# A graph layer's edge sort on one Trainium2 core: six of thirteen tiles sorted into shared places in blocks 8 to 40, sums begun later, and their one-hots made by ScalarE

## The chip, the cores and the metric

The kernel runs on one core of a Trainium2 chip. The core has five engines that run side by side, each with its own instruction stream: TensorE (PE; its weight loads are listed as PEld), VectorE (DVE), ScalarE (ACT), GpSimd (POOL) and SyncE (SP, which here only issues DMAs). They wait for one another through semaphores. SBUF is the core's working memory with 128 partitions; PSUM is the small memory that TensorE writes to. The metric is the device time of one execution in microseconds, as the median of several. Before the change it is 1903.76 us (three runs, 1901.55 to 1904.29).

## The reference: a message-passing layer over 206,250 edges

There are 6250 nodes with 64 features and 206,250 edges (in the order of `dst`) with 64 features. Cut to what matters:

```python
msg = concat([x[dst], edge_attr], axis=1)          # 206250 x 128
h = relu(msg @ W1a.T + b1a) @ W1b.T + b1b
sums = segment_sum(h, src, num_segments=6250)
agg = sums / maximum(counts, 1)[:, None]
z = relu(concat([x, agg], axis=1) @ W2a.T + b2a) @ W2b.T + b2b
out = concat([z, x], axis=1) @ Wr.T + br
result = layernorm(x + out)
```

So each edge makes a row of 128 hidden values, and the rows are summed by `src`, which is in no order. The second linear layer of the edge network is applied after the sum.

## The kernel before

**Tiles and blocks.** An edge tile is 128 edges; 13 tiles (`NG`, `BLK`) make a block; there are 124 blocks. Nodes fall into 49 bins of 128 (`NB`). The main loop (L1481) runs over blocks `k`. PE, ACT, DVE and SP run exactly in the order in which the loop's body issues their instructions (`manual_schedule`, L1468); POOL's order is left to the framework.

**A block's way.** `group` (L1138) loads, three blocks ahead, the block's edge features into the upper 64 partitions of a `rhs` buffer and the places of its `dst` nodes in a window of 64 nodes. `columns` (L1162) turns these places into one-hot columns in the lower 64 partitions, two blocks ahead, with one DVE comparison (L1171). `hidden` (L1186) multiplies tile by tile with the block's weights (TensorE) and stores the relu in `orow` (ACT, L1196), in parts of 4, 3, 3 and 3 tiles; the last part is issued later in the body than the others.

**The sort.** `bins_of` (L934) marks on DVE, two blocks ahead, which bin each edge's `src` falls into and keeps running counts by a scan (L983); two columns are carried from the block before (L969). `counts_of` (L988) adds over partitions with TensorE. `slots` (L1001) makes from this each edge's row number in DRAM. `scatter` (L1198) then sends a tile's 128 rows of 130 numbers to their places in `rows`, with one indirect DMA of POOL per tile (L1228). It is called `LEAD` = 2 blocks later.

**Joined tiles.** In blocks 5 to 103 (`joined`), the first three tiles take another way: `quads` (L1051) gives each bin's edges of these tiles whole places of four rows, `join_marks` (L1097) makes one-hot marks (DVE, L1099), `join` (L1104) moves the rows to their places with 12 matmuls (24 records) and ACT copies them into a buffer `mrow` (three of them, in `shared`), `join_places` (L1125) finds the place's index one block later, and one indirect DMA (L1203) sends all three tiles to `quads` in DRAM. Such a block has 1 + 10 scatters, others have 13.

**The sums.** Epochs of 104, 12, 4 and 4 blocks use three row buffers in turn. Once enough blocks are scattered that every bin surely has t full tiles (a step; `FULL`, `FULLQ`), SP reads those tiles back (`read`, L1285), DVE makes one-hots of the node numbers (`nodes_of`, L1310), PE sums per node (`summed`, L1332), and DVE (ACT for the first step) adds to `part` (`collect`, L1390). Groups of at most three bins or 12 tiles are spread over the blocks `LATE` = 4 after their step. `clear` (L1266) fills those places that may stay empty with padding rows, by DMAs on ACT's queue, in blocks 5 to 12 for the first epoch and the joins. `nodes_ahead` (L1451) computes the node network's part that needs no sums, four bins at a time, from block `PRE` = 14 on. Behind the last block the last sums and the node network run.

In a block's body the order is: marks, counts of the next block, three parts of `hidden`, `columns` and `bins_of` two blocks ahead, `join_places` of the last block, `nodes_ahead`, `clear`, first half of a sum, `slots` of the next block, last part of `hidden`, `join`, the rest of the sums, `scatter` of block `k - 2`.

Of the kernel before, what the change touches and what calls it, by code (L numbers as in the profile page):

```python
# [451 lines left out]
EPOCHS = (104, 12, 4, 4)  # L452
# [3 lines left out]
FULL = (4, 7, 10, 12, 15, 18)  # L456
# [6 lines left out]
PRE = 14  # L463
# [7 lines left out]
JOIN_FROM, JOIN_TO = 5, 104  # L471
FULLQ = (2, 3, 5)
# [10 lines left out]
def fast_path(  # L483
# [47 lines left out]
    DIR = BLK - JOIN  # L531
# [14 lines left out]
    def joined(k):  # L546
        return JOIN_FROM <= k < JOIN_TO
# [4 lines left out]
    def edges_of(b, n, first=0):  # L552


        tiles = sum(DIR if joined(k) else BLK for k in range(first, first + n))
# [8 lines left out]
    def quads_of(b, n):  # L564
# [4 lines left out]
        n = sum(joined(k) for k in range(n))  # L569
# [15 lines left out]
    for e, n in enumerate(EPOCHS):  # L585
# [46 lines left out]
    NREST = P * JOIN_TO  # L632
# [101 lines left out]
    with (  # L734
# [12 lines left out]
        slm = by_slot.enter_context(tc.tile_pool(name="joinp", bufs=3))  # L747
# [60 lines left out]
        nc.vector.tensor_copy(ramp, iota_i)  # L808
        in_win = steady[:, P : P + 1]
# [21 lines left out]
        starts_at(False)  # L831
# [11 lines left out]
        z_ps = steady[:, P + 2 + HALF * TJ :][:, :JOIN]  # L843
        assert DIR % 2 == 0 and DIR + JOIN == BLK == 13
# [13 lines left out]
        bases = [const.tile([P, 2 * HALF + 2], F32, name=f"bases{i}") for i in range(2)]  # L858
        most_q = const.tile([P, 1], F32, name="most_q")
        qplace = const.tile([P, JOIN_TO], F32, name="qplace")  # L860
        qidx = const.tile([P, JOIN_TO], I32, name="qidx")

        def join_consts():
# [7 lines left out]
            for t in bases:  # L871
                nc.vector.memset(t, 0.0)
            nc.vector.memset(most_q, 0.0)
            at = slp.tile([P, 1], F32, name="at")
            nc.vector.tensor_scalar(at, part_f, float(NQ), None, op0=ALU.add)
            nc.vector.tensor_scalar(qplace, ramp[:, :JOIN_TO], float(P), at, op0=ALU.mult, op1=ALU.add)
# [57 lines left out]
        def bins_of(k):  # L934
# [4 lines left out]
            if joined(k):  # L939
                return bins_joined(k, ep_, c0)  # L940
            if k == JOIN_TO:
                starts_at(False)
            oh = slp.tile([P, 2 * HALF * T], BF16, name="bins", padded_shape=[P, 2 * HALF * TJ])
            had = slp.tile([P, 2 * HALF * T], BF16, name="had", padded_shape=[P, 2 * HALF * TJ])
            by_bin = oh.rearrange("p (b t) -> p b t", t=T)
            was = none_b if k == ep_.first else state["had"][:, :, BLK]
            nc.vector.tensor_tensor(by_bin[:, :, 0], was, on[:, : 2 * HALF * T].rearrange("p (b t) -> p b t", t=T)[:, :, 1], op=ALU.mult)
# [808 lines left out]
```

## Time and profile before

| | |
|---|---|
| median of three runs | 1903.76 us (1901.55 to 1904.29) |
| the profiled execution's own time | 1908.35 us |
| its span, first to last instruction | 1906.5 us |
| instructions in the span | 31966 |
| mean granted clock of TensorE | 0.882 |
| DMA traffic | 392.17 MB, 206 GB/s on average |

A line of the page's groups, or of the view that groups by line, gives the source line, engine, operation, what is written and read (out<-in), the shape, the count, the busy microseconds, the mean nanoseconds of one, and the idle time of the engine just before it with what ended it. In the timeline a row begins with its start and length in us. In the windows view each row is a stretch of the span, with the busy us and the number of instructions of each engine, the granted share of TensorE's clock, the mean busy share of the DMA engines, and GB/s. fp32 matmuls appear as two records each. "Issue" is idle time for which the profile shows no wait.

### The profile page before, as it was taken

To read this page: it belongs to the slowest core of one execution; us is meant where nothing else is said; L and a number is where in the kernel's file an instruction comes from. 1 tells how busy PE (TensorE), PEld (TensorE's weight loads), DVE (VectorE), ACT (ScalarE), POOL (GpSimd) and SP (SyncE) were. 2 spreads that over 40 slices of the span, in tenths; PEclk is the share of its full clock that TensorE was granted. 3 is DMA by queue.
4 is the path that set the end of the run, shared out by engine and by line. 5 is a ranking of instruction groups with operands and counts; after the bars stand their busy time and mean duration, and the time that the engine had idled before them with its cause. 6 is when DMAs were issued, how large, how long until landed. Compare 5 with 4: busy or idle time off the path is not lost.

```text
span 1906.5 us, 31966 instructions
## 1 busy us (share of the span) xinstructions
PE 1450.4 (76%) x10729; PEld 1375.1 (72%) x10729; DVE 1592.4 (84%) x3348; ACT 419.1 (22%) x1203; POOL 1361.9 (71%) x1431
## 2 busy tenths in 40 slices
PE   5564677778877787787877677777788888889976
PEld 5553677768777677777777567666787887879964
DVE  7395676689998889899999888788999988898976
ACT  2221222222222222222122121212122111111035
POOL 5777776777777777777777777777777777777710
PEclk8786777788888889899899888888999999999988
DMA  8899645668665556566665545555567988888951
GB/s 191 229 350 364 215 151 168 206 193 263 199 193 163 177 173 205 168 200 207 187 195 153 158 142 164 157 169 176 184 203 222 292 251 268 246 274 273 313 155 31
DMA packets 221897, 392.17 MB, mean 206 GB/s; under 512 B 43201, under 2 KB 148020, under 8 KB 221596
## 3 DMA queue, kind: packets, MB, share of 16 engines
q1 hardware_dynamic: 139626, 227.02, 41.4%
q0 software_dynamic: 50000, 113.97, 18.3%
q10 hardware_dynamic: 32098, 49.04, 7.6%
q8 instruction: 88, 1.44, 0.3%
q14 instruction: 85, 0.70, 0.1%
HBM read 225.10 MB, written 164.77 MB: 204 GB/s over the span
## 4 chain that ended last, share of the span: by engine, by line
DVE 31%; DMA 25%; PE 24%; POOL 8%; issue 7%; ACT 2%; ACTq 2%; SPq 0%; POOLq 0%; DVEq 0%
DMA rows<-orow,rowidx 14%; PE sum_ps L1342 9%; POOL rows L1228 8%; PE h_ps L1193 7%; DMA quads<-shared,qidx 6%; DVE rhs L1171 5%; PE h_ps L1114 5%; DVE shared L1099 5%; DVE had L983 4%; DVE oh L1323 4%; DMA quads<-padrow 3%; DVE bins L977 2%; DVE part L1398 2%; DVE row L1016 1%; PE h_ps L1464 1%
## 5 line engine op out<-in xcount | busy, mean ns | idle before, releaser
L1228 POOL DMA_INDIRECT rows<-orow,rowidx x1315 | 1264.2, 961 | 427.2 <-issue 284.8
L1193 PE MATMUL h_ps<-mv,rhs 128*128 128x128 f32 x3224 | 502.3, 314 | 238.3 <-ACT of_q L1120 172.8
L1193 PEld LDWEIGHTS h_ps<-mv,rhs 128*128 128x128 f32 x3224 | 471.4, 226 | 263.5 <-ACT of_q L1120 184.7
L1342 PE MATMUL sum_ps<-rt,oh 128*128 128x129 f32 x4106 | 549.8, 291 | 83.0 <-DVE part L1398 63.2
L1342 PEld LDWEIGHTS sum_ps<-rt,oh 128*128 128x128 f32 x4106 | 523.5, 206 | 94.0 <-DVE part L1398 72.0
L1196 ACT ACTIVATE orow<-h_ps 128x512 f32<-128x512 f32 x496 | 253.0, 521 | 452.5 <-PE h_ps L1193 397.6
L1114 PE MATMUL h_ps<-orow,shared 128*128 128x130 f32 (+1 forms) x2376 | 302.0, 285 | 0.0
L1114 PEld LDWEIGHTS h_ps<-orow,shared 128*128 128x128 f32 x2376 | 295.9, 202 | 0.0
L1099 DVE TENSOR_TENSOR shared<-quad_ramp,ramp 128x1536 f32<-128x1536 f32 x99 | 173.1, 1749 | 78.5 <-PE h_ps L1114 78.5
L1171 DVE TENSOR_TENSOR rhs<-rhs,ramp 64x1664 f32<-64x1664 bf16 x116 | 219.4, 1892 | 3.6
L1118 ACT COPY shared<-h_ps 128x260 f32<-128x260 f32 x198 | 71.9, 383 | 651.8 <-DMA quads<-shared,qidx 573.3
L1323 DVE TENSOR_TENSOR oh<-ramp,rt 128x768 f32<-128x768 f32 (+2 forms) x266 | 209.7, 810 | 0.0
L1398 DVE TENSOR_TENSOR part<-part,sum_ps 128x258 f32<-128x258 f32 (+2 forms) x265 | 124.5, 470 | 72.1 <-PE sum_ps L1342 70.7
L983 DVE TENSOR_TENSOR_SCAN had<-ramp,bins 128x750 bf16<-128x750 bf16 x99 | 170.2, 1719 | 3.4
L1323 DVE TENSOR_TENSOR oh<-ramp,node 128x768 f32<-128x768 f32 (+3 forms) x133 | 118.9, 894 | 4.6
L1203 POOL DMA_INDIRECT quads<-shared,qidx x99 | 95.2, 961 | 30.2 <-issue 14.6
L997 PE MATMUL cnt_ps<-had,one_w 128*128 128x375 bf16 (+1 forms) x248 | 83.5, 340 | 42.8 <-DVE at_q L1065 34.7
L977 DVE TENSOR_TENSOR bins<-ramp,hi 128x500 bf16<-128x500 f32 x198 | 107.9, 585 | 0.0
L1016 DVE TENSOR_REDUCE row<-cnt_ps 128x10 f32<-128x500 f32 (+1 forms) x124 | 86.6, 699 | 2.3 <-PE cnt_ps L998 2.2
L998 PE MATMUL cnt_ps<-bins,before_w 128*128 128x350 bf16 (+1 forms) x248 | 84.6, 344 | 0.0
L1487 ACT CAST orow<-lo 128x13 f32<-128x13 bf16 x124 | 28.5, 230 | 249.5 <-DMA rows<-orow,rowidx 229.0
L998 PEld LDWEIGHTS <-before_w 128*128 128x128 bf16 x248 | 25.3, 102 | 56.0 <-issue 47.4
(153 smaller groups left out, 864.5 us busy)
## 6 DMA issues: line engine op xcount, KB each, us to landing
rt<-rows SPq DMA_DIRECT2D x192, 390.0 KB
rhs<-in_edgeT SPq DMA_DIRECT2D x124, 416.0 KB
rhs<-relt SPq DMA_DIRECT2D x116, 208.0 KB
rows<-orow,rowidx POOLq DMA_INDIRECT x1315
rows<-padrow ACTq DMA_DIRECT2D x4, 3900.0 KB
rt<-rows SPq DMA_DIRECT2D x48, 325.0 KB
rt<-rows SPq DMA_DIRECT2D x50, 260.0 KB
rt<-quads SPq DMA_DIRECT2D x49, 260.0 KB
```

The costliest lines, as they stand in the source:

```text
L977: nc.vector.tensor_tensor(by_bin[:, :, t0 : t0 + n], ramp[:, : 2 * HALF, None].to_broadcast([P, 2 * HALF, n]), hi[:, None, c : c + n].to_b ...
L983: nc.vector.tensor_tensor_scan(had, on, oh, 0.0, op0=ALU.mult, op1=ALU.add)
L998: nc.tensor.matmul(v[:, :, : t - 1], before_w, oh[:, b, 1:], start=False, stop=True)
L1099: nc.vector.tensor_tensor(m, quad_ramp.rearrange("p g q -> p (g q)")[:, None, :].to_broadcast([P, JOIN, QUAD * P]), z_ps[:, :, None].to_br ...
L1114: nc.tensor.matmul(ps[:, i, :w], m[:, t, (g0 + i) * P : (g0 + i + 1) * P], orow[:, t, :w], start=t == 0, stop=t == JOIN - 1,)
L1171: nc.vector.tensor_tensor(rhs[D:, :].rearrange("p (h e) -> p h e", h=2), rel, in_win[D:, :, None].to_broadcast([WIN, 2, NG * P // 2]), op= ...
L1193: done[k, c] = nc.tensor.matmul(ps[:, j, :], rhs[:, c * P : (c + 1) * P], m, start=True, stop=True).ins.name
L1196: nc.scalar.activation(orow[:, k0 : k0 + n, :H], ps[:, :n, :], AF.Relu)
L1228: s = nc.gpsimd.indirect_dma_start(out=ep_.rows, out_offset=bass.IndirectOffsetOnAxis(ap=rowidx[:, k % RING * BLK + j : k % RING * BLK + j ...
L1323: nc.vector.tensor_tensor(res[:, at_tile : at_tile + nb * n, :], ramp[:, None, :].to_broadcast([P, nb * n, P]), node[:, :, None].to_broadc ...
L1342: nc.tensor.matmul(of_bin(b), oh[:, at_tile, :], rt[:, j * n + t, : H + 1], start=t0 + t == st.lo[b], stop=t0 + t == st.hi[b] - 1,)
L1398: nc.vector.tensor_add(to, to, g.ps[:, : g.nb, :])
```

## The change

1. **Two groups in blocks 8 to 40** (`TWICE_FROM` to `TWICE_TO` - 1): `joined(k)` is now 0, 1 or 2, and such a block sorts tiles 0 to 2 and 3 to 5 into places, each with its own marks, matmuls, copies and scatter; 7 tiles go the direct way. The second marks lie in a buffer of the sums' one-hots. Five more `mrow` buffers are borrowed from the buffers of the sums' reads (`mrow_of`).
2. **The sums begin behind these blocks.** The first step is at block 38 instead of 24, and groups are issued from block 42 instead of 28. `PRE` goes from 14 to 100. The first epoch and the joins end at block 102 instead of 104.
3. **ScalarE makes the one-hots of blocks 8 to 40**, in two passes over 64 x 1664: Square(place - window row), behind the third part of `hidden`, then Relu(1 - that), between the two joins two blocks ahead.
4. **ScalarE copies the carried columns** (`carried`) for every block; DVE did it before.
5. `iota_i`, `diff_i`, `eye_b` move into borrowed memory; place numbers are computed without a table.

By the planner's formulas, which are unchanged:

| | before | after |
|---|---|---|
| steps of the first epoch, at block (tiles per bin until then) | 24 (4), 40 (7), 57 (10), 67 (12), 83 (15), 99 (18), 104 (24) | 38 (5), 56 (8), 66 (10), 77 (12), 88 (14), 98 (16), 102 (22) |
| steps of the joins | 43 (2), 59 (3), 90 (5), 104 (9) | 42 (4), 72 (6), 87 (7), 102 (11) |
| tiles surely full in epoch 0, in the joins | 19, 5 | 16, 7 |
| tiles summed in blocks 28 to 41, 42 to 49, 50 to 59 | 168, 93, 144 | 0, 134, 194 |
| 60 to 69, 70 to 79, 80 to 89, 90 to 101 | 168, 93, 82, 169 | 218, 153, 152, 158 |
| 102 to 111, 112 to 119, later | 337, 283, 418 | 281, 246, 419 |

The diff, cut to its core:

```diff
-EPOCHS = (104, 12, 4, 4)
+EPOCHS = (102, 14, 4, 4)
-FULL = (4, 7, 10, 12, 15, 18)
+FULL = (5, 8, 10, 12, 14, 16)
-PRE = 14
+PRE = 100
-JOIN_FROM, JOIN_TO = 5, 104
-FULLQ = (2, 3, 5)
+JOIN_FROM, JOIN_TO = 5, 102
+TWICE_FROM, TWICE_TO, TWICE_ROWS = 8, 41, 5
+FULLQ = (4, 6, 7)
...
     def joined(k):
-        return JOIN_FROM <= k < JOIN_TO
+        if not JOIN_FROM <= k < JOIN_TO:
+            return 0
+        return 2 if TWICE_FROM <= k < TWICE_TO else 1
...
+        def carried(k):
+            t, d = (TJ if joined(k) else T), direct(k)
+            oh = ohs[k] = slp.tile([P, 2 * HALF * t], BF16, name="bins", padded_shape=[P, 2 * HALF * TJ])
+            by_bin = oh.rearrange("p (b t) -> p b t", t=t)
+            if k == epoch_of[k].first:
+                nc.scalar.copy(by_bin[:, :, 0], none_b)
+            elif joined(k) and joined(k - 1) == joined(k):
+                nc.scalar.copy(by_bin[:, :, 0 : d + 2 : d + 1], hads[k - 1][:, :, d : d + 2])
+                return
...
         def counts_of(k, oh, had):
...
+                if joined(k) == 2:
+                    nc.tensor.matmul(of_first[:, i, :], one_w, had[:, b, direct(k) + 1 + JOIN], start=True, stop=True)
...
         def quads(k, v):
+            d, g = direct(k), joined(k)
+            of_all = v[:, :, :, TJ - 1]
+            n_i = slp1.tile([P, 2, 2, HALF], I32, name="n_i")
+            nc.vector.tensor_scalar(n_i[:, 0], of_all if g == 1 else of_first, float(QUAD - 1), None, op0=ALU.add)
+            if g == 2:
+                nc.vector.scalar_tensor_tensor(
+                    n_i[:, 1], of_all, float(2 * (QUAD - 1)), n_i[:, 0], op0=ALU.add, op1=ALU.subtract
+                )
...
+            for i in range(g):
+                nc.vector.tensor_tensor_scan(
+                    bases[:, i, 1:], ones[:, : 2 * HALF], n_i[:, i], 0.0, op0=ALU.mult, op1=ALU.add
+                )
+            for i in range(g):
+                off = offs[k, i] = slm.tile([P, 2 * HALF], F32, name="off_q")
...
+                nc.vector.tensor_tensor(cumq, n_i[:, i], cumq, op=ALU.add)
+                nc.vector.tensor_max(most_q, most_q, bases[:, i, 2 * HALF :])
+            if g == 2:
+                second = slp1.tile([P, 2, HALF], F32, name="second")
+                nc.vector.tensor_tensor(
+                    second, bases[:, 1, : 2 * HALF].rearrange("p (i b) -> p i b", i=2), of_first, op=ALU.subtract
+                )
...
+        def join_marks(k, i):
+            m = joins[k, i] = (
+                ohp.tile([P, TILES, P], F32, name="oh").rearrange("p t n -> p (t n)").rearrange("p (t q) -> p t q", t=JOIN)
+                if i else join_oh
+            )
...
+        def mrow_of(k, i):
+            q = join_at[k] + i
+            if not join_at[TWICE_FROM] <= q < join_at[TWICE_TO]:
+                return mrows[q % QROWS]
+            q %= QROWS + TWICE_ROWS
+            if q < QROWS:
+                return mrows[q]
+            return rt_all[:, READS - 1 - (q - QROWS), : QUAD * W].rearrange("p (r f) -> p r f", f=W)
...
+        def columns(g, part_of=0):
             rhs, rel, _ = made[g]
+            if g >= NEAR and joined(g) == 2:
+                of_win = rhs[D:, :].rearrange("p (h e) -> p h e", h=2)
+                if part_of == 0:
+                    nc.scalar.activation(of_win, rel, AF.Square, bias=from_win[D:, :])
+                else:
+                    nc.scalar.activation(rhs[D:, :], rhs[D:, :], AF.Relu, bias=ones[D:, :1], scale=-1.0)
+                return
+            if part_of:
+                return
...
         def scatter(k):
-            if joined(k):
+            for i in range(joined(k)):
+                q = join_at[k] + i
                 s = nc.gpsimd.indirect_dma_start(
...
-            pace = {j0: 9, 7: BLK - 1}
+            pace = {j0: 9, 7 if j0 < 6 else 9: BLK - 1}
...
             if k + 1 < NGR:
-                counts = counts_of(*ahead)
+                counts = counts_of(k + 1, *ahead)
+            if k + 2 < NGR:
+                carried(k + 2)
...
-            if joined(k):
-                join(k)
+            for i in range(joined(k)):
+                join(k, i)
+                if i == 0 and k + 2 < NGR:
+                    columns(k + 2, 1)
+            if not joined(k) and k + 2 < NGR:
+                columns(k + 2, 1)
```

More of the change, by code (lines that the diff above doesn't have):

```diff
@@ L552, in edges_of @@
     def edges_of(b, n, first=0):
-        tiles = sum(DIR if joined(k) else BLK for k in range(first, first + n))
+        tiles = sum(direct(k) for k in range(first, first + n))
         nodes = min(N, (b + 1) * P) - b * P
@@ L616, in quads_top @@
         nodes, mean, dev = quads_of(b, qep.end)
-        own = sum(own_of(b, nodes, k, 0, JOIN) for k in range(qep.first, qep.end))
+        own = sum(own_of(b, nodes, k, 0, JOIN * joined(k)) for k in range(qep.first, qep.end))
         return -(-int(mean + (own + 2 * SPREAD) / QUAD + dev + 1) * QUAD // P)
@@ L870, in join_consts @@
             )
[L871 to L872 removed]
+            nc.vector.memset(bases, 0.0)
             nc.vector.memset(most_q, 0.0)
[L874 to L876 removed]
+            for i in range(2):
+                nc.vector.tensor_scalar(qplace[:, i : i + 1], part_f, float(NQ + i * P), None, op0=ALU.add)
         def quads_now(t):
@@ L938, in bins_of @@
             c0 = k * BLK
-            if joined(k):
[L940 to L947, printed above, removed]
@@ L977, in bins_joined @@
+            if joined(k) != joined(k - 1):
+                starts_at(joined(k))
+            t = TJ if joined(k) else T
+            had = slp.tile([P, 2 * HALF * t], BF16, name="had", padded_shape=[P, 2 * HALF * TJ])
+            by_bin = oh.rearrange("p (b t) -> p b t", t=t)
+            d = direct(k)
+            for t0, c, n in ((1, c0 + BLK - d, d), (d + 2, c0, BLK - d)):
+                if n == 0:
+                    continue
                 nc.vector.tensor_tensor(
@@ new lines, in quads @@
+            for i in range(g):
+                off = offs[k, i] = slm.tile([P, 2 * HALF], F32, name="off_q")
+                nc.vector.scalar_tensor_tensor(
+                    off, bases[:, i, : 2 * HALF], float(QUAD * P * (join_at[k] + i)), cumq, op0=ALU.add, op1=ALU.subtract
+                )
[6 more added lines that the diff above has]
+                )
@@ new lines, in quads @@
+            at = slp1.tile([P, 2, HALF, 2 * JOIN], F32, name="at_q")
+            for i in range(g):
+                of = slice(i * JOIN, (i + 1) * JOIN)
+                base = second if i else bases[:, 0, : 2 * HALF].rearrange("p (i b) -> p i b", i=2)
+                nc.vector.tensor_tensor(
+                    at[:, :, :, of], v[:, :, :, d + 1 : d + 1 + g * JOIN][:, :, :, of],
+                    base[:, :, :, None].to_broadcast([P, 2, HALF, JOIN]), op=ALU.add,
+                )
+            nc.vector.tensor_reduce(
+                z_ps[:, : g * JOIN], at[:, :, :, : g * JOIN].rearrange("p i b t -> p t i b"),
+                axis=mybir.AxisListType.XY, op=ALU.max,
+            )
@@ L1477, in fast_path @@
         window(0)
-        counts = counts_of(*bins_of(0))
+        carried(0)
+        counts = counts_of(0, *bins_of(0))
         columns(0)
```

176 lines of the change are left out of this document (74 added, 102 removed).

## The prediction

> **What bounds the kernel now.** I read the page's busy shares first, then the windows view cut where the work changes, then single stretches of the timeline. The page:
>
> ```profile
> PE 1450.4 (76%) x10729; PEld 1375.1 (72%) x10729; DVE 1592.4 (84%) x3348; ACT 419.1 (22%) x1203; POOL 1361.9 (71%) x1431
> L1228 POOL DMA_INDIRECT rows<-orow,rowidx x1315 | 1264.2, 961 | 427.2 <-issue 284.8
> L1203 POOL DMA_INDIRECT quads<-shared,qidx x99 | 95.2, 961 | 30.2 <-issue 14.6
> ```
>
> By shares DVE (84%) would be the bound and POOL (71%) not. The windows view (busy us and instructions of PE, PEld, DVE, ACT, POOL; then the granted PE clock, the DMA share, GB/s) says otherwise:
>
> ```profile
> 90.00:205.00 115.00, 61.62 (x419) 57.32 (x420) 81.97 (x170) 25.50 (x74) 86.48 (x90) 0.76 1.03 356
> 205.00:420.00 215.00, 164.71 (x1029) 154.10 (x1029) 150.28 (x324) 52.67 (x148) 154.87 (x163) 0.79 0.57 173
> 420.00:1450.00 1030.00, 789.30 (x5921) 753.38 (x5920) 918.63 (x1883) 231.83 (x696) 782.01 (x815) 0.90 0.61 184
> 1450.00:1821.00 371.00, 326.00 (x2690) 316.76 (x2688) 324.04 (x607) 42.17 (x104) 280.99 (x293) 0.95 0.85 264
> 1821.00:1906.00 85.00, 58.10 (x379) 48.90 (x379) 60.56 (x258) 44.72 (x133) 0.00 (x0) 0.88 0.34 98
> ```
>
> From 420 to 1821 POOL issues a scatter every 1030/815 = 1.264 and 371/293 = 1.266 us, whatever DVE does. A scatter is 0.96 us busy, and the 0.30 us behind it ("issue" in the timeline) comes back each time:
>
> ```profile
> 620.95 0.96 POOL L1203 DMA_INDIRECT quads<-shared,qidx  x1 [0.30 <-issue]
> ...
> 634.90 0.96 POOL L1203 DMA_INDIRECT quads<-shared,qidx  x1 [0.32 <-issue]
> ```
>
> A join and ten rows take 13.95 us, and a scatter of four-row places costs what one of single rows costs. **So POOL is full at 71% busy, and the count of scatters sets the time.** The 85 us after 1821 hold no scatter and end the span in any case. Only before 420 does POOL wait for others.
>
> **The change, part by part.** The profiled execution took 1908.35 us (span 1906.5), 4.6 above the median 1903.76. I sum against it and take the same 4.6 off.
>
> *Scatters.* Before: blocks 0 to 4 and 104 to 123 have 13 each, blocks 5 to 103 have 11: 65 + 260 + 1089 = 1414, as counted above. After: 0 to 4 and 102 to 123 have 13 (351), 5 to 7 and 41 to 101 have 11 (704), 8 to 40 have 2 + 7 = 9 (297): 1352. So 62 go: 62 x 1.265 = **-78.4 us** if POOL stays full. A block of 8 to 40 then asks 9 x 1.265 = 11.39 us.
>
> *nodes_ahead moved from blocks 14 to 26 to 100 to 112.* From 205 to 420, 163 scatters need 206.2 us of 215: 8.8 are lost. Why:
>
> ```profile
> L1464 PE MATMUL h_ps<-nwzz_t,zT 128*128 128x64 f32 x98 | 23.7, 421 | 47.3 <-DVE zT L1460 47.3
> ```
>
> PE waits 47.3/13 = 3.6 us a block for DVE there, and hidden's last part and the join queue behind it. All gone: **-8.8** (bounds 0 and -8.8). In blocks 102 to 112 it meets blocks that POOL takes 13 x 1.265 = 16.4 us over, in a stage where PE and DVE are busy 88 and 87% (326 and 324 of 371 us), and where by the planner's formulas the sums fall from 337 to 281 tiles (blocks 102 to 111); I take +0, up to +10.
>
> *The clears.* The planner's caps and lows change from 24 - 19 to 22 - 16 tiles per bin in epoch 0, so each of its four clears grows by a sixth tile; those of the joins stay 4 tiles. ACT issues them between the third and the last part of hidden, and stalls:
>
> ```profile
> 175.32 11.66 ACTq L1276 DMA_DIRECT2D rows<-padrow  x2
> 187.02 0.49 ACT L1196 ACTIVATE orow<-h_ps 128x384 f32<-128x384 f32 x1 [23.73 <-DMA quads<-padrow]
> ...
> 192.25 11.03 ACTq L1276 DMA_DIRECT2D quads<-padrow  x2
> 203.33 0.49 ACT L1196 ACTIVATE orow<-h_ps 128x384 f32<-128x384 f32 x1 [10.59 <-issue]
> ```
> ```profile
> 204.09 0.96 POOL L1228 DMA_INDIRECT rows<-orow,rowidx  x1 [1.72 <-ACT shared L1118]
> ```
> ```profile
> rows<-padrow ACTq DMA_DIRECT2D x4, 3900.0 KB
> quads<-padrow ACTq DMA_DIRECT2D x4, 3120.0 KB
> ```
>
> Behind the waiting issue on ACT stand the last relu of blocks 11 and 12 (187.02 and 203.33), the join's copies, and now the next one-hots; POOL waits for the relu. Today it is late anyway and loses 1.4 us (204.09). The DMA engines are full (share 1.03), so 4 x 780 KB = 3.2 MB more add 9 to 13 us, at 356 GB/s (all traffic) or at 0.24 MB/us (the eight clears' 28 MB over that window): block 12's last relu comes at about 215, while a POOL with two scatters less in each of blocks 8 to 11 and part of 12 would be there at 191 to 193. **+21** (+11 if the drain isn't longer, +26 at most). This is the step that gives most back.
>
> *DVE in blocks 14 to 40*, where no engine has a lead on POOL any more. One block today, without sums (timeline, start to start):
>
> ```profile
> 129.59 0.67 DVE L1016 TENSOR_REDUCE row<-cnt_ps 128x10 f32<-128x500 f32 x1
> ...
> 130.38 0.20 DVE L1057 TENSOR_SCALAR n_i<-cnt_ps 128x50 int32<-128x50 f32 x1
> ...
> 130.84 0.26 DVE L1061 TENSOR_TENSOR_SCAN bases<-ones,n_i 128x50 f32<-128x50 f32 x1
> 131.14 0.31 DVE L1065 TENSOR_TENSOR at_q<-cnt_ps,bases 128x150 f32<-128x150 f32 x1
> 131.49 0.36 DVE L1070 TENSOR_REDUCE ramp<-at_q 128x3 f32<-128x150 f32 x1
> 131.76 0.20 DVE L1072 SCALAR_TENSOR_TENSOR off_q<-bases,cumq 128x50 f32<-128x50 f32 x1
> ...
> 132.19 1.75 DVE L1099 TENSOR_TENSOR shared<-quad_ramp,ramp 128x1536 f32<-128x1536 f32 x1
> 133.97 1.89 DVE L1171 TENSOR_TENSOR rhs<-rhs,ramp 64x1664 f32<-64x1664 bf16 x1
> 135.90 0.49 DVE L969 TENSOR_TENSOR bins<-had,ramp 128x100 bf16<-128x100 bf16 x1
> 136.10 1.09 DVE L977 TENSOR_TENSOR bins<-ramp,hi 128x500 bf16<-128x500 f32 x2
> ...
> 138.86 0.24 DVE L1130 SCALAR_TENSOR_TENSOR hit_q<-ramp,of_q,off_q 128x50 f32<-128x50 f32 x1
> ...
> 139.47 0.67 DVE L1016 TENSOR_REDUCE row<-cnt_ps 128x10 f32<-128x500 f32 x1
> ```
>
> It takes 9.88. Gone: the one-hots (133.97 to 135.90) 1.93, the carried columns 0.20, three columns of the row reduce 0.15. Added: second marks 1.78; in quads a second n_i 0.2, scan 0.3, off/cumq/most 0.43, at 0.35, the subtraction "second" 0.2, longer reduce and AND 0.35; in join_places a second hit and the longer tail 0.3. Sum 9.88 - 2.28 + 3.90 = **11.5 us against POOL's 11.39**. Bounds 11.0 (the small ones overlap) and 12.5 (each waits its mean); I take 11.6: 27 blocks x 0.2 = **+6** (0 to +30).
>
> *PE there* gets 24 more records. Two blocks today that carry 24 records of sums have the same load:
>
> ```profile
> 467.36 3.43 PE L1193 MATMUL h_ps<-mv,rhs 128*128 128x128 f32 x20
> ...
> 478.47 2.40 PE L1193 MATMUL h_ps<-mv,rhs 128*128 128x128 f32 x20
> ...
> 483.17 2.86 PE L1114 MATMUL h_ps<-orow,shared 128*128 128x131 f32 x24
> ...
> 489.50 0.32 PE L997 MATMUL cnt_ps<-had,one_w 128*128 128x375 bf16 x1 [2.57 <-DVE at_q L1065]
> ```
>
> From 478.47 to the next block's 489.50 PE works 8.5 us and then waits 2.57 for DVE: hidden.
>
> *ACT* gets Square and Relu over 64x1664 each. Nearest rows:
>
> ```profile
> L1196 ACT ACTIVATE orow<-h_ps 128x384 f32<-128x384 f32 x372 | 181.4, 493 | 344.7 <-PE h_ps L1193 289.8 <-DMA quads<-padrow 32.8 <-issue 18.1
> L1196 ACT ACTIVATE orow<-h_ps 128x512 f32<-128x512 f32 x124 | 75.0, 605 | 107.9 <-PE h_ps L1193 107.7
> ```
>
> 112 ns per 128 elements makes 1.6 us each. ACT's 231.83 us over the 74 blocks of 420 to 1450 are 3.1 a block; doubled, which is more than the second join's copies and the carried columns can ask, and with 3.2 of one-hots, that is 9.4 of 11.5: hidden, in the shade of DVE. Behind Square waits hidden's last relu, behind Relu the second join's copies; PE has three h_ps buffers and 1 us to spare.
>
> *The sums start at block 42, not 28.* 2053 tiles in both; by the planner blocks 60 to 69 carry 21.8 tiles and 3 groups a block, not 16.8. At 0.95/6 us a tile and 0.42 a group
>
> ```profile
> L1323 DVE TENSOR_TENSOR oh<-ramp,rt 128x768 f32<-128x768 f32 x144 | 136.8, 950 | 0.0
> L1398 DVE TENSOR_TENSOR part<-part,sum_ps 128x258 f32<-128x258 f32 x140 | 58.4, 417 | 51.0 <-PE sum_ps L1342 49.9
> ```
>
> that is 9.7 + 3.4 + 1.3 = 14.4 us against POOL's 13.9 in these ten blocks, and about 13.1 in the others to 101. A lead of a block covers 5 us: **+2** (0 to +20).
>
> Sum: -78.4 - 8.8 + 21 + 6 + 2 = -58.2. 1908.35 - 58.2 = 1850.2; less 4.6: **1845.5 us**.
>
> **Rivals.**
> 1. *DVE, not POOL, sets blocks 14 to 40* at 12.5 us or more, or the crowded sums cost their 20: for it, 11.5 against 11.39 is no margin; against it, the spacings are measured. 27 x 0.9 more is 24: 1870.
> 2. *The clears are hidden as today* (drain no longer, POOL late for other reasons): 19 less: 1826. Against it: share 1.03.
> 3. *Square isn't in ACT's loaded table*: two loads a block of 1283 ns by the row below, 2.6 us, and ACT has up to 12.0 of 11.5; if half of the loads shows, 33 x 1.3 = 43: 1888.
>
> ```profile
> L1642 ACT ACT_TABLE_LOAD x1 | 1.3, 1283 | 0.0
> ```
> The Trainium skill (ScalarE: Activation LUTs, What ACT_TABLE_LOAD costs) puts a switch of sets at about 2.66 us with its drain, and its section on table sets names relu, copy, identity and abs as fillers of every set, but not square. By that price, an estimate, ACT would need up to 14.7 us a block and the time would be up to 1950; this trace has Relu, Identity and Copy behind one load and no Square, so it can't decide.
>
> 4. *Slower: PE stays at half rate in blocks 8 to 40.* In the window 90 to 205 the granted clock is 0.76, and in the chain of waits stands a piece at
>
> ```profile
> 203.87 5.91 PE h_ps L1193 x26
> ```
>
> 0.227 us a record, where the 2.40 us above are 0.12. So 74 records make 16.8 us a block, the counts aside: 27 x 5.2 = 140 more: 1986. From 13.8 us a block on (27 x 2.2 = 59) nothing is gained. The Trainium skill (TensorE: Matmul & The Clock Gate, What's actually happening) has the clock fall after an idle window of about 3.4 us; by that rule gaps of 1 to 2 us keep PE warm and this rival needs longer ones; the 2.57 us above, behind which the next count took 0.32 us, agree.
>
> **How the numbers follow.** Likeliest 55% (1834 to 1857), rival 1 20%, rival 2 10%, rival 3 5%, slower 4%, gain nearly eaten by several of these 6%. Range 1826 to 1870. A difference under 0.2% (3.8 us) can't be told from none: faster 94%, same 2%, slower 4%.
>
> **What would show it.** 1352 scatters still 1.265 us apart; POOL idle some 20 us between 175 and 220, released by ACT behind L1276's successor; blocks 14 to 40 at 11.4 to 11.8 us; L1171's count down by 33; POOL full from block 42; last scatter near 1762, 85 us before the end. A block time above 12.5, an ACT_TABLE_LOAD per block, or POOL idle between 550 and 1000 would prove me wrong.

## The result: 1845.59 us, and the profile after

The changed kernel takes 1845.59 us (median of five runs, 1842.17 to 1846.06); the kernel before took 1903.76 beside it (five runs, 1901.55 to 1905.97). The ratio is 0.9692, 95% interval 0.9678 to 0.9706. The forecast was 1845.5. Here and below the times are medians of all runs while the ratios compare fast runs alone (a run more than 1.5% above the fastest of its kernel counts as slow), so the two can differ in the third digit.

The page of the changed kernel (busy us, share, instructions) and its view by line (count | busy, mean ns | idle time before, and what ended it):

```profile
PE 1481.3 (80%) x11539; PEld 1403.4 (76%) x11539; DVE 1588.0 (86%) x3483; ACT 614.3 (33%) x1495; POOL 1299.7 (70%) x1369
```
```profile
L1274 POOL DMA_INDIRECT rows<-orow,rowidx x1222 | 1172.5, 959 | 407.1 <-issue 270.3 <-DMA rows<-orow,rowidx 46.7 <-DVE rhs L1211 17.0
L1249 POOL DMA_INDIRECT quads<-shared,qidx x88 | 84.4, 960 | 33.8 <-issue 18.5 <-DMA rows<-orow,rowidx 3.4 <-DVE oh L1369 2.7
L1249 POOL DMA_INDIRECT quads<-rt,qidx x42 | 40.3, 959 | 16.5 <-issue 8.6 <-DMA rows<-orow,rowidx 2.1 <-ACT orow L1241 1.5
...
L1216 DVE TENSOR_TENSOR rhs<-rhs,ramp 64x1664 f32<-64x1664 bf16 x83 | 157.0, 1892 | 2.4
...
L1204 ACT ACTIVATE rhs<-rhs,from_win 64x1664 f32<-64x1664 bf16 x33 | 55.4, 1677 | 0.8
L1206 ACT ACTIVATE rhs<-rhs,ones 64x1664 f32<-64x1664 f32 x33 | 55.4, 1677 | 0.8
L732 ACT ACT_TABLE_LOAD x1 | 1.3, 1283 | 2.8 <-issue 2.8
...
L1698 ACT ACT_TABLE_LOAD x1 | 1.3, 1283 | 0.0
```

1222 + 88 + 42 = 1352 scatters, as counted; each still takes 0.96 us. DVE has lost 33 one-hots (116 to 83), and ACT has gained 66 instructions of 1.68 us. POOL is again the engine with the low busy share that sets the time, as the windows view shows (busy us and instructions of PE, PEld, DVE, ACT, POOL; granted clock, DMA share, GB/s):

```profile
90.00:205.00 115.00, 68.88 (x491) 64.46 (x491) 73.93 (x183) 50.90 (x101) 73.18 (x76) 0.78 1.03 363
205.00:420.00 215.00, 183.80 (x1580) 175.76 (x1579) 201.69 (x557) 154.88 (x295) 157.79 (x165) 0.99 0.77 234
420.00:1450.00 1030.00, 843.47 (x6591) 804.12 (x6590) 945.91 (x1909) 299.77 (x813) 781.16 (x817) 0.92 0.66 197
1450.00:1760.00 310.00, 277.10 (x2213) 266.66 (x2212) 255.63 (x491) 39.79 (x100) 233.65 (x244) 0.94 0.82 251
1760.00:1843.00 83.00, 58.12 (x379) 48.95 (x379) 60.69 (x258) 44.71 (x133) 0.00 (x0) 0.91 0.34 100
```

From 420 to 1760 it issues 1061 scatters in 1340 us, 1.263 us each: full. From 205 to 420 DVE is busy 202 of 215 us, PE does half as many records again as before (1580 against 1029) at a granted clock of 0.99 where it was 0.79, and POOL still issues 165 scatters, 1.30 us each with the end of the stall in it. POOL's first and last scatter, in the timeline of before and then of after:

```profile
16.99 1.13 POOL L1228 DMA_INDIRECT rows<-orow,rowidx  x1 [13.83 <-DVE rhs L1166]
...
1818.98 0.96 POOL L1228 DMA_INDIRECT rows<-orow,rowidx  x1 [0.30 <-issue]
```
```profile
20.11 1.13 POOL L1274 DMA_INDIRECT rows<-orow,rowidx  x1 [16.95 <-DVE rhs L1211]
...
1756.81 0.96 POOL L1274 DMA_INDIRECT rows<-orow,rowidx  x1 [0.30 <-issue]
```

The last scatter starts 62.2 us earlier, 86.9 us before the end of the span (1843.7); before it stood 87.5 ahead of the end. So the gain lies ahead of POOL's last scatter. What POOL gives back lies in the stretch of the clears. Timeline of after, ACT and POOL, with two rows of DVE:

```profile
174.66 0.49 ACT L1241 ACTIVATE orow<-h_ps 128x384 f32<-128x384 f32 x1 [0.18 <-PE h_ps L1238]
175.18 1.68 ACT L1204 ACTIVATE rhs<-rhs,from_win 64x1664 f32<-64x1664 bf16 x1
...
187.28 9.18 ACTq L1322 DMA_DIRECT2D rows<-padrow  x2
196.50 0.49 ACT L1241 ACTIVATE orow<-h_ps 128x384 f32<-128x384 f32 x1 [19.64 <-issue]
...
197.27 0.96 POOL L1274 DMA_INDIRECT rows<-orow,rowidx  x1 [14.04 <-ACT shared L1151]
...
203.99 1.72 DVE L967 TENSOR_TENSOR_SCAN had<-ramp,bins 128x750 bf16<-128x750 bf16 x1 [20.57 <-ACT bins L983]
...
205.76 0.37 ACTq L1322 DMA_DIRECT2D quads<-padrow  x1
...
206.42 0.17 DVE L1169 TENSOR_SCALAR qidx<-s_q 128x2 int32<-128x2 f32 x1
...
207.34 0.96 POOL L1249 DMA_INDIRECT quads<-shared,qidx  x1 [6.60 <-issue]
...
209.18 2.74 ACTq L1322 DMA_DIRECT2D quads<-padrow  x1
211.97 0.49 ACT L1241 ACTIVATE orow<-h_ps 128x384 f32<-128x384 f32 x1 [4.02 <-issue]
```

ACT stands 19.64 us, and the clear's DMA issue in front of its relu holds it. Of this, 10.4 us pass before the first of the two issues starts at 187.28, and 9.2 are the issues themselves. In the trace's semaphore records the first issue waits for a semaphore that the clear issued at 152.32 raises, too; the last of that clear's sixteen updates comes at 187.25. So the first half of the stall is the landing of an earlier clear. POOL, which came there sooner with its two scatters less in each block, waits 14.04 us for the join's copy behind that relu, then 6.60, and 3.44 before 221.84. For the last two the profile names no releaser; both scatters start 0.92 us after their place index (`qidx`, 206.42 and 220.92), and DVE comes to it late because its scan waited 20.57 and 2.64 us for the carried columns (L983), which ACT copies behind the held relu.

### The profile page after: what moved, and what is told of

Same layout as the page of the kernel before. It is cut to its first block, busy times and chain, and to the rows that moved or that the text cites. A ratio compares the mean times of both kernels' runs of the same rounds, so it can differ in the third digit from the quotient of the medians.

```text
span 1843.7 us, 34020 instructions
## 1 busy us (share of the span) xinstructions
PE 1481.3 (80%) x11539; PEld 1403.4 (76%) x11539; DVE 1588.0 (86%) x3483; ACT 614.3 (33%) x1495; POOL 1299.7 (70%) x1369
## 4 chain that ended last, share of the span: by engine, by line
DVE 36%; PE 25%; DMA 21%; POOL 7%; issue 7%; ACT 3%; ACTq 1%; SPq 0%; DVEq 0%; POOLq 0%
PE sum_ps L1388 13%; DMA rows<-orow,rowidx 11%; POOL rows L1274 6%; PE h_ps L1238 6%; DVE had L967 5%; DVE oh L1369 5%; DMA rows<-padrow 5%; DVE shared L1121 4%; PE h_ps L1147 3%; DVE rhs L1216 3%; DMA quads<-shared,qidx 3%; DVE bins L961 2%; DVE row L1020 2%; DVE part L1444 2%; DVE oh L1121 2%
## 5 line engine op out<-in xcount | busy, mean ns | idle before, releaser
L1274 POOL DMA_INDIRECT rows<-orow,rowidx x1222 | 1172.5, 959 | 407.1 <-issue 270.3
L1238 PE MATMUL h_ps<-mv,rhs 128*128 128x128 f32 x3224 | 433.4, 290 | 54.9 <-ACT of_q L1153 40.4
L967 DVE TENSOR_TENSOR_SCAN had<-ramp,bins 128x750 bf16<-128x750 bf16 (+1 forms) x124 | 210.5, 1697 | 102.0 <-ACT bins L983 58.0
L1369 DVE TENSOR_TENSOR oh<-ramp,rt 128x768 f32<-128x768 f32 (+4 forms) x273 | 208.8, 795 | 2.0 <-PE sum_ps L1388 0.2
L1216 DVE TENSOR_TENSOR rhs<-rhs,ramp 64x1664 f32<-64x1664 bf16 x83 | 157.0, 1892 | 2.4
L1147 PE MATMUL h_ps<-orow,oh 128*128 128x130 f32 (+1 forms) x792 | 102.5, 289 | 36.2 <-ACT orow L1241 36.2
L1444 DVE TENSOR_TENSOR part<-part,sum_ps 128x387 f32<-128x387 f32 (+2 forms) x243 | 121.0, 498 | 9.6 <-PE sum_ps L1388 9.2
L1147 PEld LDWEIGHTS h_ps<-orow,oh 128*128 128x128 f32 x792 | 98.9, 203 | 37.2 <-ACT orow L1241 37.2
L1369 DVE TENSOR_TENSOR oh<-ramp,node 128x768 f32<-128x768 f32 (+2 forms) x132 | 118.7, 899 | 4.5
L961 DVE TENSOR_TENSOR bins<-ramp,hi 128x150 bf16<-128x150 f32 (+2 forms) x221 | 115.4, 559 | 1.6
```

Of the source, the lines that this page charges most:

```text
L961: nc.vector.tensor_tensor(by_bin[:, :, t0 : t0 + n], ramp[:, : 2 * HALF, None].to_broadcast([P, 2 * HALF, n]), hi[:, None, c : c + n].to_b ...
L967: nc.vector.tensor_tensor_scan(had, on[:, : 2 * HALF * t], oh, 0.0, op0=ALU.mult, op1=ALU.add)
L1147: nc.tensor.matmul(ps[:, j, :w], m[:, t, (g0 + j) * P : (g0 + j + 1) * P], orow[:, i * JOIN + t, :w], start=t == 0, stop=t == JOIN - 1,)
L1216: nc.vector.tensor_tensor(rhs[D:, :].rearrange("p (h e) -> p h e", h=2), rel, in_win[D:, :, None].to_broadcast([WIN, 2, NG * P // 2]), op= ...
L1238: done[k, c] = nc.tensor.matmul(ps[:, j, :], rhs[:, c * P : (c + 1) * P], m, start=True, stop=True).ins.name
L1274: s = nc.gpsimd.indirect_dma_start(out=ep_.rows, out_offset=bass.IndirectOffsetOnAxis(ap=rowidx[:, k % RING * BLK + j : k % RING * BLK + j ...
```

## The experiments

One kernel, staged, ran where the kernel before took its usual time; it is told first, and the conclusions rest on it and on the two traces. The others ran on chips on which the kernel before itself took 2540 to 2630 us, so that they say nothing of the gain at 1904; they are told behind it, for what they do say.

### staged: three questions in one profile

One kernel, read by stages: PE's work is cut down, DVE makes the one-hots of blocks 8 to 27 and ACT those of 28 to 40, and the first eight clears come later. The edit is cut here: angle brackets stand for longer expressions, and the like cuts in the joins and the sums are left out.

```diff
-                for j in range(n):              # hidden: one matmul a tile
-                    done[k, c] = nc.tensor.matmul(ps[:, j, :], rhs[:, c * P : (c + 1) * P], m, ...)
+                last = nc.tensor.matmul(ps[:, 0, :], <bf16 half of rhs tile k0>, <bf16 half of m>, ...)
-            if g >= NEAR and joined(g) == 2:
+            if g >= NEAR and joined(g) == 2 and g >= 28:
-EARLY = 14
+EARLY = 54
-        clears = {5 + 2 * i: (0, i) for i in range(CLEAR)}
+        clears = {41 + 3 * i: (0, i) for i in range(CLEAR)}
-        clears.update({6 + 2 * i: (-1, i) for i in range(CLEAR)})
+        clears.update({42 + 3 * i: (-1, i) for i in range(CLEAR)})
```

> The changed kernel with PE's work cut to what the places of the rows need (it leaves out most of the products: hidden makes one 128-column bf16 matmul a part and ScalarE reads it for all of the part's tiles, a join three and one of 131 columns, the sums one a read; every scatter, copy, one-hot, wait and load stays), so that PE should be off the path on a chip that holds it back, and two edits that are read in different stages of the one profile. In blocks 8 to 27 DVE makes the one-hots, in blocks 28 to 40 ACT does; the eight first clears stand at blocks 41 to 51 instead of 5 to 12 (their scatters follow from block 54). Theory A (POOL's count sets the time, 0.4 us below it comes DVE's block of 10.95, and ACT's waiting DMA issues made the stall): blocks 14 to 27 take 12.7 to 13.1 us each, set by DVE, and POOL loses 1.3 to 1.7 a block; blocks 28 to 40 take 11.3 to 11.5, POOL full; no gap of POOL over 2 us between 170 and 225 us that ACT's clears release; from block 54 on 13.9 us a block of 11 scatters. Theory B (POOL has slack in the twice-joined blocks, or the stall was the full DMA engines): blocks 14 to 27 within 0.3 us of blocks 28 to 40, and a stall of 10 us or more left before 225 us. If PE still sets all blocks alike, at over 13 us in 28 to 40 too, only the clears are tested.

It took 1857.78 us (1856.86 to 1858.93) beside 1908.78, ratio 0.9735 (0.9718 to 0.9751). Windows of it (the trace holds no clock record before 1054 us, so that the clocks of the first three rows and of half the fourth say nothing):

```profile
90.00:205.00 115.00, 29.84 (x159) 16.26 (x160) 109.16 (x244) 37.74 (x120) 87.20 (x90) 1.00 0.46 127
330.00:490.00 160.00, 47.76 (x261) 26.91 (x261) 152.07 (x405) 97.24 (x206) 118.02 (x124) 1.00 0.68 202
556.00:722.00 166.00, 32.74 (x156) 16.79 (x154) 120.17 (x240) 37.74 (x121) 107.23 (x112) 1.00 1.02 344
722.00:1376.00 654.00, 179.98 (x934) 108.63 (x935) 621.89 (x1244) 153.95 (x487) 496.18 (x518) 0.76 0.68 198
```

*PE is not what sets the time.* With PE at 28% of the stretch from 722 to 1376 the scatters come 654/518 = 1.263 us apart, as in the changed kernel with PE at 82%. Freeing an engine that already kept up gained nothing there.

*DVE's margin is as small as the prediction said.* Timeline of staged, the row reduce of two blocks that follow each other and POOL's waits beside them:

```profile
262.40 0.96 POOL L1251 DMA_INDIRECT quads<-rt,qidx  x1 [3.22 <-DVE qidx L1168]
...
275.01 0.52 DVE L1020 TENSOR_REDUCE row<-cnt_ps 128x7 f32<-128x350 f32 x1
...
288.02 0.52 DVE L1020 TENSOR_REDUCE row<-cnt_ps 128x7 f32<-128x350 f32 x1
...
288.39 0.96 POOL L1251 DMA_INDIRECT quads<-shared,qidx  x1 [3.23 <-DVE qidx L1168]
```

With the one-hots on DVE a block takes 13.01 us, DVE without a gap. POOL needs 11.37 for its nine scatters; once its backlog is worked off, from 254 us on, it stands 2.9 us at the place index of every second block and 0.34 behind it, 1.6 us a block; as it had the backlog first, POOL loses 16 us in all in these blocks, not 1.6 in each. In blocks 28 to 40 the same kernel, with the one-hots on ACT, gives

```profile
375.04 0.51 DVE L1020 TENSOR_REDUCE row<-cnt_ps 128x7 f32<-128x350 f32 x1
...
523.56 0.67 DVE L1020 TENSOR_REDUCE row<-cnt_ps 128x10 f32<-128x500 f32 x1
```

148.52/13 = 11.42 us a block as DVE's mean (10.9 to 11.3 in eleven of them, 14.20 and 13.22 in the last two), and POOL's timeline shows no wait there. Theory A gave 12.7 to 13.1, 1.3 to 1.7 and 11.3 to 11.5. So the move of the one-hots to ACT is no ornament: with PE cut down as here, it is worth 1.6 us a block once POOL has caught up.

*The stall at the clears goes with the clears, but as much comes back.* Without them the DMA engines' share from 90 to 205 falls from 1.03 to 0.46, POOL issues 90 scatters there and not 76, and between 107 and 241 us no scatter comes more than 0.3 us later than the usual 1.265 behind the last. But at blocks 44 to 53 it now stands 8.9, 7.5 and 8.0 us, 24.4 together, where the changed kernel lost 23.7 between 170 and 225. This was not forecast. The waits of staged between 580 and 612 us (in all, times, longest), around the first of the three:

```profile
PE sum_ps L1391 <- DVE oh L1371: 18.3, 3, 9.8
ACT orow L1241 <- PE h_ps L1235: 15.0, 2, 9.0
DVE oh L1371 <- DMA rt<-rows: 11.5, 2, 10.8
POOL quads L1251 <- ACT bins L983: 9.2, 1, 9.2
ACT bins L983 <- DVE had L967: 5.5, 2, 2.9
```

DVE's one-hots of a sum wait 10.8 us for rows that are read back; DVE's own later work and PE, which runs in order too, come late by it, then ACT, and POOL behind an ACT copy that itself waited for DVE's scan. The second stall looks alike. The third is ACT behind a clear's issue again:

```profile
703.37 0.34 ACTq L1324 DMA_DIRECT2D quads<-padrow  x1
703.76 0.49 ACT L1241 ACTIVATE orow<-h_ps 128x384 f32<-128x384 f32 x1 [22.20 <-DMA rhs<-in_edgeT]
...
704.52 0.95 POOL L1276 DMA_INDIRECT rows<-orow,rowidx  x1 [8.29 <-ACT orow L1241]
```

ACT stands 22.20 us, and what ends it is the landing of a load that SP issued: by the same records the clear's issue waits for a semaphore that this load raises. All three fall where the clears, some 31 MB (4 of 4680 and 4 of 3120 KB) in eleven blocks, and the loads share full DMA engines (1.02 from 556 to 722). So in this move the transfer kept its price, partly through late loads and partly through ACT's held issue. That the two sums are so near each other is not explained: from block 42 on the sums' reads want the DMA engines too. Clears spread over more blocks ran only where PE is held back (below).

Both edits account for staged's longer time: POOL's waits beyond the usual, summed over all scatters, are 44.1 us in staged and 30.5 in the changed kernel; the difference of 13.6, less the first scatter's start 1.2 us earlier, is to 0.4 that of the spans (1855.7 - 1843.7 = 12.0).

### Where PE is held back

All ran with the kernel before beside them. `e1_single` is the change without its second group; `light_after` and `light_late` let the matmuls of hidden, joins and sums read only the upper 16 bits of each word; `no_pe_after` leaves out most products from block 8 on. A ratio above 1 means slower than the kernel before.

```diff
 e1_single        -TWICE_FROM, TWICE_TO, TWICE_ROWS = 8, 41, 5
                  +TWICE_FROM, TWICE_TO, TWICE_ROWS = 8, 8, 5
                  -FULL = (5, 8, 10, 12, 14, 16)     FULLQ = (4, 6, 7)
                  +FULL = (6, 9, 12, 14, 16, 18)     FULLQ = (3, 4, 5)
 e2_late_clears   -EARLY = 14      clears at 5 + 2 * i and 6 + 2 * i
                  +EARLY = 52      clears at 35 + 4 * i and 37 + 4 * i
 e3_dve_onehots   -if g >= NEAR and joined(g) == 2:
                  +if g >= NEAR and False:
 e4_pre14         -PRE = 100
                  +PRE = 14
 light_...        -nc.tensor.matmul(ps[:, j, :], rhs[:, c * P : (c + 1) * P], m, ...)
                  +nc.tensor.matmul(ps[:, j, :], rhs[...].bitcast(BF16)[:, 1::2], m.bitcast(BF16)[:, 1::2], ...)
 twice49_all      -TWICE_TO = 41   FULL = (5, 8, 10, 12, 14, 16)  FULLQ = (4, 6, 7)
                  +TWICE_TO = 49   FULL = (6, 8, 10, 12, 14)      FULLQ = (5, 7, 8)
                  +one-hots of every block from 8 on by ACT, clears as in e2_late_clears
```

e1_single: 

> The changed kernel without the second group: blocks 5 to 101 join one group of three tiles (13 + 10 rows less, 11 scatters a block), DVE makes all one-hots, but nodes_ahead stays at blocks 100 to 112 and the sums still begin late (block 39). It issues 1418 scatters. Theory A (POOL's count of scatters sets the time): 66 x 1.265 = 83 us more than the changed kernel, less some 10 of its wait at the clears: 1895 to 1908 us, within 0.5% of the kernel before, scatters 1.265 us apart, DVE busy above 1590. Theory B (the gain came from the moved nodes_ahead and the later sums): below 1870 us.

e2_late_clears: 

> The changed kernel with the eight clears of the first epoch's rows and of the joins moved from blocks 5 to 12 to blocks 35 to 49, and the scatters that must follow them from block 14 to 52. Theory A (POOL's 23.7 us idle between 176 and 225 us are the relus and copies behind ACT's waiting DMA issues): 18 to 24 us less, 1822 to 1828 us, at most 5 us of new gaps after 420 us. Theory B (the DMA engines are full there with other loads, and POOL comes late in any case, or the stall only moves to blocks 35 to 49): 1838 us or more.

e3_dve_onehots: 

> The changed kernel with the first-layer one-hots of blocks 8 to 40 on DVE again, at their 1.89 us a block; all else stays. Theory A (DVE's block of 10.95 us is only 0.4 below POOL's 11.36 for nine scatters): DVE's block is 12.8 to 12.9 and sets blocks 14 to 40: 27 x 1.45 = 39 us more, 1880 to 1890 us, POOL idle 1.4 us a block there. Theory B (DVE's queue has slack, and its waits swallow the 1.9 us): below 1856 us.

e4_pre14: 

> The changed kernel with nodes_ahead at blocks 14 to 26 again, not at 100 to 112. Theory A (PE waits 3.6 us a block for DVE in it, and a block of 11.4 us has no room for it): 13 x 2.5 to 3.6 = 33 to 47 us more, 1878 to 1893 us. Theory B (it costs what it cost before, where a block took 14.2): 9 to 11 us more, 1855 to 1857. Theory C (hidden in both places): 1846.

after_again, the changed kernel itself: 

> The changed kernel itself, unaltered, beside the kernel before, as a control: on three calls the kernel before took 2540 to 2630 us and its variants 2620 to 2670, with PE held up by gaps of about 0.35, 0.7 and 1.4 us that no semaphore explains. Theory A (the gain hangs on POOL being full, and there PE is what is full): where the kernel before takes over 2500 us the changed kernel loses, 1 to 4% slower, as its 24 more matmuls a block in blocks 8 to 40 then count; where it takes 1904 us, the ratio is 0.969. Theory B (the change's gain does not hang on PE's rate): ratio 0.98 or less on either chip.

light_after: 

> The changed kernel with the matmuls of hidden, of the joins and of the sums reading only the upper 16 bits of each word as bf16, so that each is one PE record, not two (the numbers lose their lower halves; every other instruction, wait and transfer stays). Theory A (POOL's count of scatters sets the time, and PE bounds it only where PE is held back): within 15 us of 1845, 1830 to 1850, also on a chip where the kernel before takes 2550; scatters 1.26 us apart through blocks 14 to 123. Theory B (what is slow on those chips isn't PE's own rate): above 2100 us there. Theory C (PE's time is on the path on a good chip too): below 1820.

light_late: 

> The same with PE relieved in the same way, and with the eight clears of the first epoch's rows and of the joins moved from blocks 5 to 12 to blocks 35 to 49 (the scatters that must follow them from block 14 to 52). Theory A (POOL's 23.7 us idle between 176 and 225 us are the relus and copies behind ACT's waiting DMA issues): 18 to 24 us less than light_after of the same call, no gap of POOL over 2 us between 170 and 225 us, at most 5 us of new ones at blocks 35 to 49. Theory B (the DMA engines are full there anyway, or the stall only moves): within 8 us of it.

no_pe_after: 

> The changed kernel with nearly all PE work of the per-edge part taken out from block 8 on, and every scatter, copy, one-hot, wait and load left in: hidden makes one matmul a part, not three or four, each join 4, not 12, the sums one a read, all in bf16 (it leaves out most of the products; the places of the rows stay right). It is meant for the chips on which the kernel before takes 2550 to 2620 us because PE is held up. Theory A (POOL's count of scatters sets the changed kernel's time where PE keeps up; 20 us of start, 1352 x 1.264, 24 us of stall at the clears, and the tail, which loses PE work too): 1810 to 1850 us, POOL's scatters 1.26 us apart from block 14 on with under 10 us of gaps behind 230 us, and the stall of 20 to 28 us between 170 and 225 us, released by ACT. Theory B (POOL is not the bound even then; DVE or the transfers are): over 1900 us with POOL's gaps spread over the blocks.

twice49_all: 

> Three edits on the changed kernel: twice-joined blocks 8 to 48 (eight more, 16 scatters fewer: 1336; the sums' full steps re-chosen, so that the first comes at block 50), the one-hots of every block from 8 on made by ACT (1.9 us a block off DVE), and the eight first clears at blocks 35 to 49. Theory A (POOL's count, 1.265 us a scatter, and the stall at the clears are what is left of the time), where the kernel before takes its 1904 us: -20 for the scatters, -20 for the stall, 0 to +10 for the sums crowded into fewer blocks: 1805 to 1820 us. Theory B (DVE or PE, not POOL, sets blocks 42 to 101 once the sums are denser): 1835 or more. Where the kernel before takes over 2500 us, PE decides and neither is tested: 2580 to 2680.

| kernel | us | before, beside it | ratio (95%) |
|---|---|---|---|
| e1_single | 2619.05 | 2541.57 | 1.029 (1.021 to 1.038) |
| e2_late_clears | 2623.93 | 2541.57 | 1.034 (1.027 to 1.041) |
| late_clears, late_clears_2: the same edit on two other chips | 2673.08, 2619.70 | 2630.51, 2539.07 | 1.018 (1.011 to 1.025), 1.030 (1.025 to 1.035) |
| e3_dve_onehots | 2625.02 | 2541.57 | 1.034 (1.027 to 1.041) |
| e4_pre14 | 2649.91 | 2541.57 | 1.041 (1.034 to 1.049) |
| after_again | 2623.50 | 2550.12 | 1.035 (1.027 to 1.044) |
| twice49_all | 2662.61 | 2622.58 | 1.014 (1.008 to 1.020) |
| light_after | 2209.48 | 2621.87 | 0.841 (0.838 to 0.844) |
| light_late | 2212.16 | 2621.87 | 0.842 (0.839 to 0.846) |
| no_pe_after | 2159.21 | 2542.42 | 0.848 (0.842 to 0.855) |

What follows is little, and none of it is a measure of the terms. The changed kernel loses about 3% there: the scatters it saves are worth nothing where POOL waits. The window of after_again that stands beside the one of after shows it: 115 scatters and not 165, 1036 PE records and not 1580.

```profile
205.00:420.00 215.00, 155.67 (x1036) 141.56 (x1036) 136.32 (x378) 98.85 (x196) 110.04 (x115) 0.82 0.57 184
```

My reason for the loss, the 24 more matmuls a block, does not hold: e1_single does not have them and loses 2.9% too. It shares with the change the later sums, nodes_ahead at the end, the shorter first epoch and ACT's carried columns. e4_pre14 puts nodes_ahead back and is no faster for it (2649.91), so its place alone isn't the reason; the others no run parts. e1, e2 and e3 lie within 6 us of each other, so neither the second group, nor the clears, nor the place of the one-hots decides anything there.

Cutting PE's records to 55% (light_after) takes some 410 us off the 2623.5 of after_again, on another chip; that is about half of what lies above the usual 1846. Theory A's 1830 to 1850 failed, and theory B's "above 2100" came. A cut to a quarter (no_pe_after) gives no better a ratio (0.848 against 0.841), and theory A's 1810 to 1850 failed there too; theory B's "over 1900" came. So PE's work is about half of what is slow there, and the rest is not explained. The moved clears change nothing (light_late against light_after, 2.7 us more). twice49_all was meant as a better version than the change; it lies within 2% of the kernel before there (1.014), was never seen at 1904, and stays open.

## Why the prediction was right, point by point

By spans the gain is 1906.5 - 1843.7 = 62.8 us, where the sum gave 58.2; by medians it is 58.2. The difference is the 4.6 us by which the profiled execution of before lay above its median; the one of after is itself the median (1845.59). So that the forecast falls on the tenth is partly luck: between the two traces the sum was 4.6 too cautious, and what made that good was that the execution profiled before lay above its median by as much. Within the sum, errors of several us cancel, too.

POOL's own account from the two timelines, term by term (a wait is what a scatter's start lies more than 1.27 us behind the last one's). The rows must add up to the spans' difference, as they cut one stretch of time into pieces; what they show is where it lies. Which edit caused a row is read from the timelines, as no run at the usual time has one edit less:

| term | forecast | found |
|---|---|---|
| 62 scatters | -78.4 | -78.4, by the count; spacing 0.002 shorter, cause not known: -2.8 over 1351 |
| nodes_ahead out of blocks 14 to 26 | -8.8 | -10.8: eight waits of before between 290 and 400 us are gone |
| clears | +21 | +22.3: 23.7 us of waits where 1.4 were |
| DVE in blocks 14 to 40 | +6 | at most +1.7: three waits, at 304.5, 306.4 and 370.1, of which DVE ends one (0.6) and earlier scatters' DMAs two |
| crowded sums | +2 | 0: waits of 0.15 in all behind 420 us |
| nodes_ahead at 100 to 112 | 0 | 0 |
| start and first blocks | none | +3.1 (first scatter at 20.11, not 16.99), +2.7 of waits before 170 us |
| behind the last scatter | 0 | -0.7 |
| sum | -58.2 | -62.9, spans -62.8 |

- *What bounds the kernel* was read rightly: the count of scatters, at 70% busy. staged adds that PE can be cut from 82% to 28% busy without a change in the spacing. A run with the scatters' number alone changed would show it most directly; e1_single was meant for that, and it ran only where PE is held back.
- *The clears* were the largest loss and came in the main as put: ACT's relu behind its waiting DMA issue, and POOL idle behind that. The forecast of 215 us for block 12's last relu was 211.97. But POOL already stands at block 11's relu (196.50) and loses most there, and 9.4 of the 23.7 us come by a path that the step didn't name, DVE's scan behind ACT's carried columns. Nor did it say what staged showed, that the price of the transfers came back at blocks 44 to 53.
- *DVE's block* was mis-sized: 11.5 was the estimate, and the timeline of after has

```profile
297.82 0.52 DVE L1020 TENSOR_REDUCE row<-cnt_ps 128x7 f32<-128x350 f32 x1
...
308.75 0.51 DVE L1020 TENSOR_REDUCE row<-cnt_ps 128x7 f32<-128x350 f32 x1
```

10.93 us. The lower bound, 11.0, was the true end. The sum took the distances of starts in before for the new instructions, and these came out shorter:

```profile
301.91 1.75 DVE L1121 TENSOR_TENSOR shared<-quad_ramp,ramp 128x1536 f32<-128x1536 f32 x1
303.58 1.75 DVE L1121 TENSOR_TENSOR oh<-quad_ramp,ramp 128x1536 f32<-128x1536 f32 x1
305.24 0.90 DVE L961 TENSOR_TENSOR bins<-ramp,hi 128x350 bf16<-128x350 f32 x2
```

The two marks take 1.67 and 1.66 us from start to start, not 1.78 each (0.23 less together), quads' additions 1.64 and not 1.83, join_places' 0.26 and not 0.3, and `bins_of` saves 0.12 beyond its carried columns, since it now has 7 direct tiles (128x350, before 128x500); I had left that out. So DVE's block stays 0.4 below POOL's 11.37, hardly anything of the +6 is left, and rival 1 is dead. That it would cost if DVE were longer was right: with 1.9 us more on DVE (staged) POOL loses 1.6 a block once its backlog is gone.
- *ACT's one-hots* are 1.68 us each (1.6 estimated), in the shade of DVE as said, and there are two table loads in the whole kernel, none per block: rival 3 is dead. The Trainium skill (ScalarE: Activation LUTs, its section on table sets) doesn't name square as a filler of every set; this trace has Square and Relu alternate 33 times without a load, and the measurement decides.
- *Rival 4* (PE at half rate in blocks 8 to 40) did not come: granted clock 0.99 from 205 to 420, with PE idle for 3.43 us once and otherwise never over 1.9 us at a time. Before, it stood 3.56 to 4.46 us thirteen times in this window, at a clock of 0.79. The Trainium skill's rule that the clock falls after an idle window of about 3.4 us (TensorE: Matmul & The Clock Gate, What's actually happening) agrees with both rows. Where PE is held back the change is about 3% slower, but as e1_single loses as much without the second group, this is not rival 4's mechanism.
- *What I left out*: the start. The first scatter goes out 3.1 us later than before, and the early blocks wait 2.7 more. The timelines of before and of after show where the 3.1 come from:

```profile
6.59 1.61 DVE L954 TENSOR_TENSOR_SCAN had<-ramp,bins 128x700 bf16<-128x700 bf16 x1
```
```profile
11.10 0.40 ACT L981 COPY bins<-none_b 128x50 bf16<-128x50 bf16 x1
...
11.53 1.61 DVE L967 TENSOR_TENSOR_SCAN had<-ramp,bins 128x700 bf16<-128x700 bf16 x1 [5.00 <-ACT orow L1534]
```

The carried columns of block 0 now stand on ACT, behind its copy of PE's first product (L1225, 10.81), and DVE's scan has to wait for them; DVE made them itself before. The counts and the first one-hots of L1211 come 3.1 us later by it (14.56, before 11.44). The sum had this move as 0.2 us saved on DVE and put the wait at nothing. No run has the carried columns back on DVE. The 5.8 of start and early blocks nearly cancel what DVE's block and the sums cost less (6.3).

## What to carry to other kernels

Find the engine whose start-to-start time is constant, whatever its busy share, and count its instructions: each one saved was worth its period here, less what the shortened engine then waits for elsewhere. A cost that is a transfer (a clear, a fill) need not go away when its issue is moved: the one move that ran at the usual time paid as much in the new place, and spreading it over many more blocks is untried there. An instruction that goes to another engine ties the two queues together: 0.2 us saved on DVE made its first scan wait 5.00 us for ACT. And check the distances of starts that you carry over from another place: they depend on the neighbours (1.67 us for marks that took 1.78).

## What the runs showed of the hardware that I had not expected

The same kernel before took 1903.76 and 1908.78 us in two series of runs and 2540 to 2630 in the others; the chip of one number gave 2541.57 and later 1908.78. In the others, PE's results come long after the matmuls that the trace shows. In the timeline of light_after:

```profile
706.54 1.27 PE L1239 MATMUL h_ps<-mv,rhs 128*128 128x128 bf16 x10
...
715.10 1.36 ACT L1242 ACTIVATE orow<-h_ps 128x512 f32<-128x512 f32 x3 [11.92 <-remote]
```

The relus that wait for these ten matmuls start 7.3 us after the trace has them end. DVE, which needs PE's counts, starts its row reduce within 0.05 us of them (715.05), released by the same unnamed source. The other engines' instructions keep their durations (a scatter 0.96 us, the one-hots 1.89). The Trainium skill (TensorE: Matmul & The Clock Gate, Seeing it yourself) warns that recorded clock events are unreliable and that a clock stuck at a quarter has been seen; a deeper throttle than the mean clocks on record (0.80 in after_again, 0.60 in light_after) would fit, but no run here shows it, and the cause stays open.

Second, a scatter's period hardly depends on what it moves: in the changed kernel the next scatter starts 1.264 us after one of four-row places of 2080 bytes and 1.263 us after one of single rows of 520, and a block with nine scatters runs as evenly as one with eleven.
